# A four-layer graph network on one core: layer 2's first maxima formed beside layer 1's sums, part of the neighbour counts moved into layer 1, and the stores moved to another queue

## The chip, the cores and the metric

The kernel runs on one core of one Trainium2 chip. The metric is the time of one execution on the device in microseconds (us). The kernel before takes 3031.22 us (median of three runs, 3029.73 to 3033.5).

A core has five engines, each with its own instruction stream[...]: PE (matrix multiply, with a separate stream of weight loads), DVE (vector), ACT (scalar functions), POOL (general) and SP (here only the issue of transfers). ACT and POOL issue transfers too. The 16 DMA engines move the data. [...]

## The reference, cut to what matters

There are N = 4096 nodes with D = 256 features and a 4096 x 4096 int32 adjacency matrix with about 0.8% ones. Each layer normalises each row, takes `relu`, applies a graph operation and adds the result to `x`.

```
for layer in 0..3:   h = relu((x - mean) / sqrt(var + eps));   x = x + layer(h)

layer 0: attention over neighbours (leaky slope 0.2), a wide dense part, a gate, a norm
layer 1: a = (adj == 1);  deg = a.sum(axis=1);  (a @ h / deg) @ W.T + b
layer 2: g = h @ W;  src = g @ a[:D];  dst = g @ a[D:]
         e = src[:,None] + dst[None,:];  e = where(e > 0, e, 0.01 * e)
         elu(softmax(where(adj > 0, e, -1e12), axis=1) @ g)
layer 3: Q, K, V = h@Wq, h@Wk, h@Wv;  softmax(Q K^T + mask(adj + I)) @ V
```

In layer 2 the row maximum of the masked `e` only needs, for each row, the largest `dst` among its neighbours, because the leaky function rises everywhere.

## The kernel before, in words

The rows are cut into NT = 32 tiles of 128 rows; four tiles make a block (`BT` = `RB` = 4), so there are NB = 8 blocks. All of `x` stays on the chip as `xs`. The order of the instructions on each engine is set by the framework's scheduler, which takes the program's order as priority; the order named here is that of the built kernels. Pools with few buffers and releases of memory add waits.

**Layer 0** first runs an attention (`class Attention`), which also turns the adjacency into transposed codes and stores them in DRAM (`codesT`, one MB for each block of four row tiles and each quarter of the columns). Then comes its dense part (`dense`, lines 691 to 850), a generator for each block of rows; two blocks are in flight. `with_counts` runs a `count` (lines 681 to 692) after each step: POOL loads a 128 x 1024 piece of the adjacency as bf16 (`ask`, line 681, four buffers), and ACT reads it twice with a Sign function whose sum goes to `over` (line 689). There are 128 pieces and 256 signs; from them comes `deg`. `turn` transposes on PE, and its result is taken out of PSUM by DVE (`onto`, line 644) or ACT (`nc.scalar.copy`, line 641). `measure1` takes mean and deviation of the finished rows for layer 1, with one POOL power (line 117).

**Layer 1** (lines 862 to 938) starts with `opening`: the last four blocks of `h @ W.T` (`halves1`), in a high and a low half. `gather(t)` then loads the codes of row tile t through SP (line 902, four buffers `code`), compares them with one value on DVE (line 907, two buffers `eq` of the whole width), sums with 32 matrix products on PE (line 911, two PSUM buffers `acc`), and adds the mean to `xs` (ACT line 918, DVE lines 920 to 922).

**Layer 2** (lines 941 to 998) begins when layer 1's memory is free. POOL loads W and a (lines 187 and 194), and DVE forms W a from them (line 202). For each block, `block2` normalises (`preln`, ACT line 134), transposes (line 145) and projects (`project`, line 154, ACT line 215), which gives g, src and dst together. `reach(n)` (lines 236 and 238) takes two column tiles of the running maximum of dst over the neighbours: DVE subtracts and takes the minimum on a 128 x 512 tile in PSUM. At a block's last n it turns the result, forms two rows, and sends them through DRAM to get them to all partitions (`ab_d`, `ab_row`, lines 271 and 272). `run` then goes over eight row blocks and 16 pairs of column tiles: DVE makes `y` (line 284), POOL subtracts the code (line 288), ACT takes the exponential (line 315), PE sums (line 326). `reach` of the next block runs among them, LEAD = 3 pairs ahead.

**Layer 3** goes over 16 pairs of row tiles; `fetch3` loads codes through SP (line 1079), and the results go out through POOL (line 1177).

Of the kernel before, what the change touches and what calls it, by code (L numbers as in the profile page):

```python
# [21 lines left out]
P = 128  # L22
# [19 lines left out]
def kernel(ctx: ExitStack, tc: tile.TileContext, w: dict, out: bass.AP):  # L42
# [114 lines left out]


# [6 lines left out]
    class Attention:  # L165
        def __init__(self, outer, es, tag, slope, lag, n_y, blocks, turned, finish, side="left"):
# [3 lines left out]
            vp = outer.enter_context(tc.tile_pool(name=f"{tag}_v", bufs=1, side=side))  # L170
            self.v = vp.tile([P, NT, D + 3], F32, name="v")
            nc.gpsimd.memset(self.v[:, :, 0:1], 1.0)
            vp = es.enter_context(tc.tile_pool(name=f"{tag}_sd", bufs=1))
            self.sdst = vp.tile([P, NT], F32, name="sdst")
            self.cdst = vp.tile([P, NT], F32, name="cdst")
            self.ab_d = [
# [6 lines left out]
            self.ps_top = es.enter_context(tc.tile_pool(name=f"{tag}_top", bufs=1, space=PSUM))  # L183
        def weights(self, wp, work, wm, a_srcs, eng):
# [23 lines left out]
        def project(self, b, hT, psm, rs=None):  # L208
# [9 lines left out]
            at = ts(b, BT)  # L218
            dst = self.v[:, at, D + 2]
# [3 lines left out]
        def reach(self, n):  # L223
# [8 lines left out]
            for j in range(c, c + 2):  # L232
                code = self.turned(b, j // QT)[:, :, j % QT, :]
                dst = self.v[:, j, D + 2 : D + 3]
                if j == 0:
                    nc.vector.tensor_scalar(st["run"], code, dst, None, ALU.subtract)
                else:
                    nc.vector.scalar_tensor_tensor(  # L238
                        st["run"], code, dst, st["run"], ALU.subtract, ALU.min
                    )  # L240
            if c < NT - 2:
                return
# [98 lines left out]
    def measure1(small, b):  # L341
        at = ts(b, BT)
        mv = small.tile([P, BT, 2], F32, tag="pl_mv", name="pl_mv")
        for i in range(BT):
            stats_of(small, xs[:, b * BT + i, :], mv[:, i, :], "pl")
        rs = rstd_of(small, mv, BT, "pl", stats1[:, 0, at])
        nc.vector.scalar_tensor_tensor(
            stats1[:, 1, at], mv[:, :, 0], -1.0, rs, ALU.mult, ALU.mult
# [32 lines left out]
    with ExitStack() as l0:  # L381
# [10 lines left out]
        with ExitStack() as es:  # L392
# [18 lines left out]
            att = Attention(v0, es, "l0", 0.2, 3, 8, cuts, turned_of, finish0, "right")  # L411
# [192 lines left out]
        with ExitStack() as es:  # L604
            d = es.enter_context(tc.tile_pool(name="l0_d", bufs=1))
            AHEAD = 4
# [68 lines left out]
            asked, came = [(t, q) for t in range(NT) for q in range(NQ)], []  # L675

            def ask(n):
                for t, q in asked[len(came) : n]:

                    came.append(code_p.tile([P, QW], BF16, tag="a", name="a", bufs=AHEAD))  # L680
                    nc.gpsimd.dma_start(out=came[-1], in_=adj[ts(t, P), ts(q, QW)])

            def count(g):

                ask(g + AHEAD - 1)
                t, q = asked[g]
                for v in range(2):
                    sign = code_p.tile([P, QW], BF16, tag="sign", name="sign", bufs=1)
                    nc.scalar.activation(  # L689
                        sign, came[g], AF.Sign, bias=limits[:, v : v + 1],  # L690
                        accum_out=over[:, t, v, q : q + 1],
                    )

            def dense(b):
# [8 lines left out]
                for k in range(KD):  # L703
                    turn(
                        whT[:, k, :], [wh[:, b * BT + i, ts(k, P)] for i in range(BT)],
                        onto if k else nc.scalar.copy,
# [42 lines left out]
                turn(abT, [dt[:, i, :] for i in range(BT)], nc.scalar.copy)  # L749
# [87 lines left out]
                if b < NB - 1:  # L837
                    measure1(small, b)
# [18 lines left out]
            def with_counts(b):  # L857
                at, n = b * BT * NQ, BT * NQ
                for k, _ in enumerate(dense(b)):
                    if k < n:  # L860
                        count(at + k)
                    yield

            ask(AHEAD - 2)
            run_staggered([with_counts(b) for b in range(NB)], 16)

    with ExitStack() as es:  # L870

        code_p = es.enter_context(tc.tile_pool(name="l1_code", bufs=4))
        eq_p = es.enter_context(tc.tile_pool(name="l1_eq", bufs=2))
# [8 lines left out]
        psm = es.enter_context(tc.tile_pool(name="l1_psm", bufs=3, space=PSUM))  # L882
        ps_acc = es.enter_context(tc.tile_pool(name="l1_acc", bufs=2, space=PSUM))

        def block1(b):
            if b == NB - 1:
                measure1(small, b)
            h = work.tile([P, BT, D], F32, tag="h", name="h")
            hT = work.tile([P, KD, BW], F32, tag="hT", name="hT")
# [4 lines left out]
        nc.vector.tensor_reduce(sums, over, AX.X, ALU.add)  # L894
        rdeg = vp.tile([P, NT], F32, name="rdeg")
        nc.vector.tensor_tensor(rdeg, sums[:, :, 0], sums[:, :, 1], ALU.subtract)
        nc.vector.tensor_scalar(rdeg, rdeg, 0.5, None, ALU.mult)
        nc.vector.reciprocal(rdeg, rdeg)
        def gather(t, parts=1):
# [6 lines left out]
            eq = eq_p.tile([P, N], F32R, tag="eq", name="eq")  # L906
            nc.vector.tensor_scalar(eq, code, UNIT, None, ALU.is_equal)  # L907
            yield
            acc = ps_acc.tile([P, 2 * D], F32, tag="acc", name="acc")
            for c in range(NT):  # L910
                nc.tensor.matmul(  # L911
                    out=acc, lhsT=eq[:, ts(c, P)], rhs=v1[c // BT][:, c % BT, :, :],
# [9 lines left out]
            nc.vector.tensor_tensor(xs[:, t, :], xs[:, t, :], o, ALU.add)  # L922

# [17 lines left out]
    with ExitStack() as es:  # L941
        work2 = es.enter_context(tc.tile_pool(name="l2_work", bufs=2))

        minus = const.tile([P, 1], F32, name="minus")
        nc.gpsimd.memset(minus, -1.0)

        def finish2(at, accs, rden):

            h = work2.tile([P, RB, D], F32, tag="hp", name="hp")
            for r, acc in enumerate(accs):  # L950
                by = rden[:, r : r + 1]
                if r % 2:
                    nc.vector.tensor_scalar(
                        h[:, r, :], acc[:, 1 : D + 1], by, -1.0, ALU.mult, ALU.add
                    )
                else:
# [275 lines left out]
```

## Time and profile before

The profiled execution took 3033.89 us; its span, from the first to the last instruction, is 3032.1 us.

| Stage | from, us | to, us | PE busy, us | ACT busy, us | DVE busy, us | POOL busy, us |
|---|---|---|---|---|---|---|
| layer 0, attention | 0 | 625 | 569.5 | 351.9 | 402.8 | 368.6 |
| layer 0, dense part | 625 | 1239 | 576.8 | 496.3 | 288.0 | 275.2 |
| layer 1, opening | 1239 | 1285 | 40.0 | 18.5 | 21.0 | 7.1 |
| layer 1, sums | 1285 | 1507 | 221.8 | 14.8 | 125.8 | 6.0 |
| layer 2, before its first sum | 1507 | 1576 | 42.0 | 31.9 | 49.1 | 7.1 |
| layer 2, attention | 1576 | 2057 | 463.0 | 199.9 | 364.3 | 278.4 |
| layer 3 | 2057 | 3032 | 963.6 | 162.0 | 602.2 | 22.4 |

The table is read from the profile's stretches: the busy time of each engine between two moments of the span. A stage in which PE is busy nearly throughout can be shortened only by letting PE do less or wait less. In a group of the profile, a name such as `L911 PE acc` is a line of the code, an engine and what is written[...]. "DMA share" is the part of a stretch in which the 16 DMA engines had a packet in hand.

### The profile page before, as it was taken

What the parts mean: (1) busy time and instruction counts of PE and PEld (TensorE: products, weight loads), DVE (VectorE), ACT (ScalarE), POOL (GpSimd) and SP (SyncE); (2) the same over time, 40 slices, a digit from 0 to 9 for tenths busy, and PEclk for the clock granted to TensorE, in tenths of its full rate; (3) what the DMA queues carried; (4) which work ended last, traced back from release to release, by engine and by line L of the source; (5) the groups of instructions that cost most, each with busy time, mean ns of one, the idle gap of its engine ahead of it and who ended that gap; (6) DMA issues with size and microseconds to landing.
All of it is one profiled execution on the core that took longest, in us unless ns stands there. A gap on an engine that the chain in (4) does not pass through costs nothing.

```text
span 3032.1 us, 34952 instructions
## 1 busy us (share of the span) xinstructions
PE 2876.7 (95%) x13353; PEld 2343.2 (77%) x13353; DVE 1853.2 (61%) x3304; ACT 1275.3 (42%) x1944; POOL 964.7 (32%) x750
## 2 busy tenths in 40 slices
PE   6999999999899999899969999999999999999999
PEld 5778888866565665788758887888888888888887
DVE  5876666425444444455588878745766566566653
ACT  5766555369999972410144344443212111111211
POOL 4676665535544443100025565550000000000000
PEclk9999999999999999999979999999999999999999
DMA  6966655244444430244222222101111111111100
GB/s 144 213 146 126 140 122 141 57 69 74 77 77 75 75 53 8 97 149 147 84 105 87 84 77 77 49 18 60 63 34 61 39 34 61 35 37 61 34 7 8
DMA packets 105824, 235.21 MB, mean 78 GB/s; under 512 B 10716, under 2 KB 27096, under 8 KB 97464
## 3 DMA queue, kind: packets, MB, share of 16 engines
q0 software_dynamic: 39232, 73.30, 15.8%
q1 hardware_dynamic: 63752, 157.04, 15.0%
q10 hardware_dynamic: 2672, 2.62, 0.3%
q8 instruction: 105, 1.72, 0.2%
q14 instruction: 63, 0.52, 0.1%
HBM read 262.22 MB, written 37.81 MB: 99 GB/s over the span
## 4 chain that ended last, share of the span: by engine, by line
PE 39%; issue 31%; ACT 10%; POOL 7%; DVE 7%; DMA 4%; POOLq 0%; ACTq 0%; SPq 0%; DVEq 0%
PE acc L326 18%; PE acc L911 8%; PE mm L154 7%; POOL y L288 4%; ACT sign L689 4%; PE s L154 3%; DVE run L238 3%; PE acc L1164 2%; DVE y L284 2%; DMA ab_row<-l_ab_d 1%; DMA a<-in_adj_dram 1%; ACT y L315 1%; ACT zT L667 1%; ACT turned L449 1%; ACT t L656 1%
## 5 line engine op out<-in xcount | busy, mean ns | idle before, releaser
L326 PE MATMUL acc<-v,y 128*128 128x257 f32 x4096 | 938.0, 387 | 35.3 <-ACT hp L957 17.0
L326 PEld LDWEIGHTS acc<-v,y 128*128 128x128 f32 x4096 | 778.0, 193 | 152.0 <-ACT hp L957 21.8
L288 POOL TENSOR_TENSOR y<-y,turned 128x1024 f32<-128x1024 f32 (+1 forms) x272 | 550.1, 2035 | 339.0 <-DVE y L284 298.4
L315 ACT ACTIVATE y<-y,sdst 128x512 f32<-128x512 f32 (+1 forms) x544 | 350.7, 689 | 365.1 <-POOL y L288 364.8
L284 DVE SCALAR_TENSOR_TENSOR y<-ab_row,cdst,b 128x512 f32<-128x512 f32 (+1 forms) x544 | 368.2, 710 | 166.5 <-PE acc L326 108.1
L1164 PE MATMUL acc<-v,y 128*128 128x257 f32 x2048 | 454.5, 380 | 0.4 <-DVE rden L1172 0.4
L154 PE MATMUL s<-qT,hT 128*128 128x256 f32 x2048 | 445.2, 379 | 0.7 <-ACT qT L1112 0.7
L1157 ACT ACTIVATE y<-y 128x1024 f32<-128x1024 f32 x128 | 132.2, 1055 | 714.3 <-DVE y L1156 710.0
L154 PEld LDWEIGHTS s<-qT,hT 128*128 128x128 f32 x2048 | 389.0, 190 | 54.2 <-ACT qT L1112 1.4
L1164 PEld LDWEIGHTS acc<-v,y 128*128 128x128 f32 x2048 | 387.1, 190 | 55.9 <-issue 0.8
L238 DVE SCALAR_TENSOR_TENSOR run<-turned,v,run 128x512 f32<-128x512 bf16 (+1 forms) x527 | 379.5, 720 | 61.1 <-DMA turned<-codesT 27.0
L1177 POOL DMA_DIRECT2D out_dram<-o x32 | 17.3, 542 | 936.5 <-DVE rden L1172 933.0
L689 ACT ACTIVATE sign<-a,limits 128x1024 bf16<-128x1024 bf16 x256 | 294.0, 1148 | 16.9 <-DMA a<-in_adj_dram 11.0
L1126 DVE SCALAR_TENSOR_TENSOR y<-code,s 128x512 f32<-128x512 bf16 x256 | 175.7, 687 | 100.6 <-PE s L154 100.3
L1156 DVE TENSOR_TENSOR y<-y,top 128x1024 f32<-128x1024 f32 x128 | 146.2, 1214 | 43.0 <-PE top L1150 43.0
L1133 DVE TENSOR_TENSOR mx<-mx,y 128x512 f32<-128x512 f32 x224 | 154.8, 691 | 7.5
L449 ACT ACTIVATE turned<-cT,log_wide 128x1024 bf16<-128x1024 bf16 x128 | 141.1, 1102 | 31.7 <-PE cT L444 31.3
L154 PE MATMUL mm<-kept 128*128 128x512 f32 x288 | 137.4, 612 | 8.8 <-ACT kept L641 7.5
L911 PE MATMUL acc<-early,eq 128*128 128x512 f32 x512 | 127.1, 400 | 4.3 <-DVE early L372 2.5
L907 DVE TENSOR_SCALAR eq<-code 128x4096 fp32r<-128x4096 bf16 x32 | 73.4, 2294 | 81.6 <-PE acc L911 78.8
L911 PE MATMUL acc<-late,eq 128*128 128x512 f32 x512 | 122.7, 391 | 0.0
L911 PEld LDWEIGHTS acc<-early,eq 128*128 128x128 f32 x512 | 96.9, 190 | 27.8 <-DVE early L372 2.8
(224 smaller groups left out, 2951.3 us busy)
## 6 DMA issues: line engine op xcount, KB each, us to landing
adj_t<-in_adj_dram POOLq DMA_DIRECT2D x128, 256.0 KB, 4.7
codesT<-turned SPq DMA_DIRECT2D x32, 1024.0 KB
a<-in_adj_dram POOLq DMA_DIRECT2D x128, 256.0 KB, 4.2
code<-codesT SPq DMA_DIRECT2D x128, 256.0 KB
turned<-codesT SPq DMA_DIRECT2D x32, 1024.0 KB
code<-codesT SPq DMA_DIRECT2D x64, 512.0 KB
ab_row<-l_ab_d SPq DMA_DIRECT2D x15, 512.0 KB
xt<-in_x_dram SPq DMA_DIRECT2D x8, 512.0 KB
```

The lines of the kernel that those rows point to most:

```text
L154: nc.tensor.matmul(out=ps, lhsT=lhsT_of(k), rhs=rhs_of(k), start=(k == 0), stop=(k == n - 1))
L238: nc.vector.scalar_tensor_tensor(st["run"], code, dst, st["run"], ALU.subtract, ALU.min)
L284: nc.vector.scalar_tensor_tensor(y[:, :, k, :], st["ab"][:, 0, :, :], self.cdst[:, c + k : c + k + 1], st["b"], ALU.add, ALU.max,)
L288: nc.gpsimd.tensor_tensor(y, y, mask[:, :, c % QT : c % QT + 2, :], ALU.subtract)
L315: nc.scalar.activation(y[:, :, k, :], y[:, :, k, :], AF.Exp, bias=self.sdst[:, c + k : c + k + 1],)
L326: nc.tensor.matmul(out=acc, lhsT=y[:, r, k, :], rhs=self.v[:, c + k, 0 : D + 1], start=(c + k == 0), stop=(c + k == NT - 1),)
L449: nc.scalar.activation(ct.rearrange("p c i -> p (c i)"), ps, AF.Exp, scale=math.log(UNIT / WIDE), bias=log_wide,)
L689: nc.scalar.activation(sign, came[g], AF.Sign, bias=limits[:, v : v + 1], accum_out=over[:, t, v, q : q + 1],)
L911: nc.tensor.matmul(out=acc, lhsT=eq[:, ts(c, P)], rhs=v1[c // BT][:, c % BT, :, :], start=(c == 0), stop=(c == NT - 1),)
L1126: nc.vector.scalar_tensor_tensor(y[:, :, c : c + 2, :], st["code"][:, :, c : c + 2, :], -BIG / UNIT, ps, ALU.mult, ALU.add,)
L1133: nc.vector.tensor_tensor(mx, mx, y[:, :, c : c + 2, :], ALU.max)
L1164: nc.tensor.matmul(out=accs[r], lhsT=st["y"][:, r, c, :], rhs=v3[:, c, :], start=(c == 0), stop=(c == NT - 1),)
```

## The change

- **Counts.** `Tally` replaces `ask` and `count`. Twenty-two row tiles (`COUNTED`) are counted in layer 0's dense part, 11 pieces for each block in place of 16; the last ten tiles (40 pieces, 80 signs) are counted in layer 1, written in `gather(t)` for the tiles t up to 27. `deg` of these ten is formed tile by tile (`degrees`).
- **Dense part.** DVE takes both halves of `whT` and `abT` out of PSUM; ACT took `abT` and one half of `whT` before.
- **Layer 1.** `code` has two buffers in place of four, `eq` is split into two halves with three half buffers in place of two whole ones, and one PSUM buffer `mm` is given up (three to two), as layer 2's `run` and `top` are now held in layer 1.
- **Layer 2's dst.** After each fourth row tile of layer 1, `reach2(b)` measures the four finished tiles, normalises them on ACT (`normed2`), and lets DVE form dst as a product with the vector W a (`wa2`, spread over all partitions by two matrix products in `weights2`) and a sum along the row. It then takes the two `reach` steps of row block 0 that these columns allow; the codes for it come through SP into one buffer (`stored1`). After block 6 the normalised and turned rows of blocks 0 and 1 (`hT2`) are made.
- **Layer 2's start.** `project` no longer waits for any of this and no `reach` of block 0 is left; `top(0)` finishes block 0's maxima after its projection.
- **Stores.** SP issues the 32 stores of the result in place of POOL.

```diff
+        def count(self, g):
+            self.ask(g + self.bufs - 1)
+            t, q = self.asked[g]
+            for v in range(2):
+                sign = self.pool.tile([P, QW], BF16, tag="sign", name="sign", bufs=1)
+                nc.scalar.activation(
+                    sign, self.came[g], AF.Sign, bias=limits[:, v : v + 1],
+                    accum_out=over[:, t, v, q : q + 1],
+                )
...
-                        onto if k else nc.scalar.copy,
+                        onto,
...
-                turn(abT, [dt[:, i, :] for i in range(BT)], nc.scalar.copy)
+                turn(abT, [dt[:, i, :] for i in range(BT)], onto)
...
-        code_p = es.enter_context(tc.tile_pool(name="l1_code", bufs=4))
-        eq_p = es.enter_context(tc.tile_pool(name="l1_eq", bufs=2))
+        code_p = es.enter_context(tc.tile_pool(name="l1_code", bufs=2))
+        eq_p = es.enter_context(tc.tile_pool(name="l1_eq", bufs=3))
+        over_a = es.enter_context(tc.tile_pool(name="l1_a", bufs=AHEAD))
...
-            eq = eq_p.tile([P, N], F32R, tag="eq", name="eq")
-            nc.vector.tensor_scalar(eq, code, UNIT, None, ALU.is_equal)
+            eqs = []
+            for half in range(2):
+                eqs.append(eq_p.tile([P, N // 2], F32R, tag="eq", name="eq"))
+                nc.vector.tensor_scalar(
+                    eqs[-1], code[:, ts(half, N // 2)], UNIT, None, ALU.is_equal
+                )
+            for g in range(t * n_late // BESIDE, min((t + 1) * n_late // BESIDE, n_late)):
+                tally.count(g)
+                if g % NQ == NQ - 1:
+                    at = COUNTED + g // NQ
+                    degrees(slice(at, at + 1))
...
+            if t % BT == BT - 1:
+                reach2(t // BT)
...
+        def reach2(b):
+            if b == 0:
+                weights2()
+            measure(small, b, stats2)
+            for i in range(b * BT, b * BT + BT):
+                h = two2.tile([P, D], F32, tag="hd", name="hd")
+                normed2(h, i)
+                junk = two2.tile([P, D], F32, tag="junk", name="junk")
+                nc.vector.tensor_tensor_reduce(
+                    junk, h, wa2[0], 1.0, 0.0, ALU.mult, ALU.add, att2.own_dst[:, i : i + 1]
+                )
+            att2.slopes(ts(b, BT))
+            for n in range(2 * b, 2 * b + 2):
+                att2.reach(n)
+            if b == NB - 2:
+                for k in range(2):
+                    hT2[k] = turn2(k, pst)
...
             def block2(b):
-                h = work.tile([P, BT, D], F32, tag="h", name="h")
-                preln(small, xs[:, ts(b, BT), :], h)
-                yield
-                hT = transposed_block(work, pst, h, "hT")
+                hT = hT2.pop(b) if b in hT2 else turn2(b, pst)
                 yield
-                att.project(b, hT, psm)
+                att2.project(b, hT, psm)
                 yield
-                for n in range(2 * b, 2 * b + 2 if b < NB - 1 else PPB + LEAD):
-                    att.reach(n)
-
-            run_staggered([block2(b) for b in range(NB)], 2)
-
-        att.run(es, LEAD, 5)
+            blocks = [block2(b) for b in range(NB)]
+            for _ in blocks.pop(0):
+                pass
+            att2.top(0)
+            run_staggered(blocks, 1)
+            for n in range(PPB, PPB + LEAD):
+                att2.reach(n)
+        att2.run(es, LEAD, 5)
...
-                nc.gpsimd.dma_start(out=out[ts(t, P), :], in_=o)
+                nc.sync.dma_start(out=out[ts(t, P), :], in_=o)
```

## The prediction

> **What bounds the kernel now.** I read the stretches of the span first, stage by stage, then the chain that ended last between 1507 and 1641 us, then single groups.
>
> ```profile
> 625.00:1239.00 614.00, 576.80 (x2132) 370.72 (x2131) 288.00 (x643) 496.25 (x793) 275.19 (x254) 0.97 0.40 63
> 1285.00:1507.00 222.00, 221.75 (x961) 180.43 (x962) 125.76 (x199) 14.82 (x37) 6.04 (x6) 1.00 0.41 124
> 1507.00:1576.00 69.00, 41.99 (x200) 33.66 (x199) 49.12 (x98) 31.93 (x71) 7.07 (x7) 0.79 0.31 122
> ```
>
> Columns: stretch, length, busy us of PE, weight loads, DVE, ACT, POOL, then granted clock, DMA share, GB/s. PE sets the time almost everywhere. The hole is the third stretch: from layer 1's last sum to layer 2's first, PE works 42 of 69 us at a clock of 0.79. The chain tells why:
>
> ```profile
> 1507.09 0.89 PE tp L145 x8
> 1511.23 9.84 DMA a<-in_L_gnn_a_dram
> 1522.09 13.07 PE mm L154 x48
> 1550.92 3.66 PE mm L154 x16
> 1556.02 0.77 DVE run L238
> 1570.75 1.41 DVE y L284 x2
> 1572.46 2.13 POOL y L288
> 1574.61 0.73 ACT y L315
> 1575.39 34.48 PE acc L326 x144
> ```
>
> Layer 2's weights come late (PE resumes at 1522), eight blocks are projected until 1558, and only then do block 0's maxima end. Turning them, two transfers and y take until 1575.39.
>
> **The change, part by part.**
>
> *Layer 2's start.* Removed from here: the weights' load and the `reach` steps of block 0. What stays on PE: eight projections of 3.66 us (the x16 row) and six turned blocks of 0.89 us, 34.6 us. Before, the eight projections with five turned blocks among them took 1522.09 to 1558.06, 36.0 us, so the eight need 36.9 with the sixth. ACT is nearly as full: 32 row copies at 0.38, 24 `relu` at 0.55, six evictions at 0.59 and four late `relu` for the last tiles make 31 us. Those four wait for the last tiles' deviation (below) with PE's evictions queued behind them; I add 1.5 us. With the first y's exponential 1.5 more: 1507 + 36.9 + 1.5 + 1.5 = 1546.9, against 1575.4. **-28.5 us.**
>
> The other path must be shorter. After the last sum: mean added (0.37 + 0.42 + 0.48 + 0.42, with hops 2.0), deviation (0.43 + 0.18 + 0.17 + POOL 1.02 + 0.16, with hops 2.4), `relu` and four row sums (3.0), four `reach` at 0.77 (3.1): 1517.5. From there the old tail, from the end of `run` (1559.4) to PE's start (1575.4), is 16 us. The row's two transfers go through SP behind loads of codes (1520 to 1530: DMA share 1.01 at 427 GB/s), 3 to 5 us more. Row ready and exponential possible at about 1537 to 1539, 8 us before PE is free. So y runs further ahead than before, which bears on the end of layer 2's first row block:
>
> ```profile
> 1630.00:1640.00 10.00, 6.03 (x28) 4.94 (x26) 7.33 (x16) 6.98 (x11) 10.00 (x5) 0.98 0.30 105
> 1640.00:1650.00 10.00, 9.80 (x31) 8.07 (x32) 6.41 (x8) 4.20 (x7) 4.41 (x3) 0.68 0.14 48
> 1650.00:1660.00 10.00, 10.00 (x47) 8.76 (x47) 8.19 (x12) 4.00 (x6) 6.07 (x4) 1.00 0.14 60
> ```
>
> PE gets 28 and 31 records through where 47 is normal: 35 records, 7.4 us, lost because DVE was not ahead. Eight more us of lead could remove all of it or, if DVE spends them on evictions, nothing. I take half: **-4 us** (0 to -7).
>
> *Dense part.* Per block here: 40 signs in the built order, before and after, until they run out. A sign takes 1.148 + 0.190 us, in a row one each 1.27.
>
> ```profile
> L689 ACT ACTIVATE sign<-a,limits 128x1024 bf16<-128x1024 bf16 x256 | 294.0, 1148 | 16.9 <-DMA a<-in_adj_dram 11.0
> 879.60:954.30 74.70, 70.67 (x258) 45.47 (x257) 34.97 (x80) 69.16 (x112) 37.26 (x36) 0.95 0.49 77
> 1104.60:1175.50 70.90, 68.01 (x255) 44.33 (x254) 35.69 (x80) 33.05 (x52) 27.02 (x17) 0.98 0.07 15
> ```
>
> Moving 80 signs takes 80 x 1.27 = 102 us from ACT, but PE is busy 70.7 of 74.7 us beside them. With few signs left a block takes 70.9 to 71.6, with 40 it takes 75.1 (mean of the five intervals between the table loads ahead of zT from 708 to 1084). The signs end after 4.4 intervals in place of 6.4, so two intervals are shortened: 2 x 3.5 = 7 us. The evictions moved to DVE (16 at 0.69) spare ACT's delay (PE waited 0.9 us for each) where signs stand in front, and where none do they lengthen PE's wait for whT (2.3 us at 1127.7) by about 0.7: +1. **-6 us** (-18 to +3).
>
> *Layer 1's opening.* DVE's first instruction for layer 2's weights stands ahead of the first eq, and waits for W and a through POOL. `w_L_gnn_WT`, issued at the same place before, took 7.8 us; alone, a load of this size took 3.2. So that eq starts at 1248 to 1253 (1247.4 before), with eight evictions queued behind. The half eq (1.15) gives back 1.1; two `mm` buffers for three and 16 signs among the ACT evictions cost up to 1.27 a step. **+2 us** (-1 to +8).
>
> *Layer 1's sums.* PE needs 7.41 us a tile (222/30). DVE for four tiles: eq 9.2, mean and statistics 7.7, degrees 1, `reach2` 6, together 24 of 29.6 us. A half eq may begin 7.4 us ahead of its use; going through DVE's order at a `reach2`, the latest half is done 3 us early. ACT: signs come at 20 to 21 for four tiles, 26 us, with `lo` and `relu` 31 of 29.6, until the 80 are gone at about tile 13. `lo` waits behind them, and PE for `lo`, but a sum has two buffers, 5 us of slack: nothing yet. POOL's powers queue behind its loads, and those wait for signs, which only passes the same lag on.
>
> The scarcest is DMA. One piece costs 1.75 us of the 16 engines (0.49 x 74.7, less 1.5 for x, over 20 pieces), a code tile 3.5 (0.47 x 7.41), `stored1` 0.4. Per tile 2.6 x 1.75 + 3.5 + 0.4 = 8.4 against 7.41: 1.0 x 12 tiles = 12 us, less 5 for the two sums and 3 for the four piece buffers. **+4 us** (0 to +14). SP's four new loads wait for the previous one's use, issued a block earlier; the first waits for layer 0's memory with code tile 2 behind it, needed 35 us later.
>
> [...]
>
> ```profile
> L907 DVE TENSOR_SCALAR eq<-code 128x4096 fp32r<-128x4096 bf16 x32 | 73.4, 2294 | 81.6 <-PE acc L911 78.8 <-DMA code<-codesT 2.9
> ```
>
> [...] Before, POOL issued nothing beside it, [...] I take 0.
>
> *Stores.* SP's fetch in layer 3 comes once in 56 us, and stores ahead of it are done by then: nothing. At the end POOL's second issue came at 3028.63, 2.5 us after the first ended, and landed 2.0 later; SP issues at its own 0.4 each: **-2.5 us** (-4 to 0).
>
> **Sum.** -28.5 - 4 - 6 + 2 + 4 - 2.5 = -35 against the profiled span of 3032.1, 2997; its own execution took 3033.9, 2.7 above the median of the runs. From 3031.2: **2996 us.**
>
> **Rivals.**
> - *The lag in layer 1 reaches PE.* For it: the 8.4 us, and everything from `lo` to the powers in one line. If neither buffers help nor the opening: +12, +8, +8 in place of +6: 3012 to 3022, I say 3014. Against it: 93% of ACT and 59% of DMA time there is free today. 0.18.
> - *More gain.* All of the 7.4, a start at PE's 34.6, and dense -15: 2977. For it: slower PE clock after each wait (0.95 in the dense intervals). Against it: whT's wait is DVE's. 0.20.
> - *Layer 2's start stays bound.* The row arrives after the projections, behind the loads in SP's queue, or ACT's order holds PE: first sum at 1556, 3005 to 3009. 0.12.
> - *Slower.* Code loads share the DMA engines with the pieces, with two buffers for four. If each of 13 tiles waits for its code, layer 1 decides at 35/13 = 2.7 us a tile, 10.1 us: a code load (4.4 us at 1242.9) would have to take over 12 us from eq to eq. At 11.5 us a tile: 3050. 0.04.
> - *The signs do not move or the weights stay late*: the built order shows both moved; 0.01.
>
> **How the numbers follow.** The case of the sum has 0.45, and its own range is 2986 to 3006. With the rivals, 2976 to 3015 leaves 0.2 out. Faster by over 0.2% (about what three runs of this kernel tell from no change: below 3025) 0.93, within it 0.03, slower 0.04.
>
> **What would show it.** Layer 2's first sum about 40 us after layer 1's last (69 before), at full clock. Layer 1's 30 tiles in 222 to 230 us, DMA share near 1 and ACT full until tile 13. Dense intervals of 75 for four, then 71. Last store issued by SP within 1 us of DVE. The prediction is wrong if PE waits in layer 1 for `lo` or eq at every tile, or if PE's stop at 1630 stays.

## The result, and the profile after

The changed kernel takes 2998.55 us (median of four runs, 2995.66 to 3001.03); the kernel before took 3030.47 us beside it (four runs). The ratio is 0.9894, 95% interval 0.9882 to 0.9906. The forecast was 2996 us, with a range of 2976 to 3015. The profiled execution of the changed kernel took 2998.89 us; its span is 2997.0, against 3032.1 before: 35.1 us less, where the sum of the prediction had 35. By the medians the gain is 31.9 us; the profile of before was one of the slower executions (3033.89 us), and that the two sums agree to 0.1 us is chance.

The agreement says little about the terms. To see them, the span is cut at events that both kernels have: the first table load of ACT inside the dense part, the last tanh of the dense part, the first and the last sum of layer 1, the first and the last sum of layer 2, and the first scores of layer 3.

| Stage, us | before | after | change | predicted |
|---|---|---|---|---|
| layer 0 up to the first table load | 651.6 | 648.4 | -3.2 | 0 |
| dense part, first table load to last tanh | 577.6 | 562.7 | -14.9 | -6 |
| layer 1's opening, last tanh to first sum | 21.2 | 26.0 | +4.8 | +2 |
| layer 1's sums | 256.7 | 261.0 | +4.3 | +4 |
| layer 2's start, last sum of layer 1 to first of layer 2 | 68.3 | 40.2 | -28.1 | -28.5 |
| layer 2, first to last sum | 480.2 | 480.2 | 0.0 | -4 |
| layer 3's opening, to its first scores | 44.8 | 50.2 | +5.4 | not in the sum |
| layer 3's scores, sums and stores | 931.8 | 928.4 | -3.4 | -2.5 |
| span | 3032.1 | 2997.0 | -35.1 | -35 |

So the large term held, and five others were off by 2.8 to 8.9 us, with signs that cancel. These are the stretches of the changed kernel that answer to those shown of before (stretch, length, busy us of PE, weight loads, DVE, ACT, POOL, then granted clock, DMA share, GB/s):

```profile
606.90:1220.90 614.00, 584.68 (x2203) 376.31 (x2202) 297.69 (x659) 392.70 (x616) 253.81 (x216) 0.99 0.29 46
1271.80:1498.30 226.50, 224.93 (x987) 182.53 (x986) 162.19 (x364) 109.97 (x203) 29.08 (x37) 1.00 0.66 178
1498.10:1538.30 40.20, 35.40 (x182) 29.61 (x180) 36.74 (x68) 29.59 (x69) 4.66 (x4) 1.00 0.50 196
1568.30:1578.30 10.00, 5.76 (x29) 4.74 (x28) 8.79 (x17) 4.26 (x7) 4.57 (x3) 0.97 0.21 75
1578.30:1588.30 10.00, 10.00 (x41) 8.49 (x40) 8.26 (x12) 0.59 (x1) 0.64 (x1) 0.86 0.25 84
852.20:927.00 74.80, 70.50 (x259) 44.21 (x257) 37.84 (x82) 69.44 (x110) 38.10 (x38) 0.98 0.51 78
996.50:1066.30 69.80, 67.90 (x257) 43.29 (x256) 36.02 (x82) 21.46 (x31) 26.26 (x16) 1.00 0.02 8
```

The reader sees ACT lose 104 us of work in the dense part (496.3 to 392.7) and gain 95 in layer 1 (14.8 to 110.0). Layer 2's start is 40.2 us long at full clock, with PE busy in 35.4 of them. A dense interval without signs takes 69.8 us. And the stop of PE near the end of layer 2's first row block, 28 and 31 records where 47 are normal before (each of these products leaves two records, 4096 for the 2048 of L368), is still there: 29 and 41.

The chain that ended last, over the new start of layer 2 (start us, us, engine, tile, line):

```profile
1496.94 1.15 PE acc L1006 x5
...
1500.89 1.01 POOL stats L117
...
1502.12 1.09 ACT hd L934 x2
...
1503.53 3.76 PE mm L154 x16
...
1508.55 0.44 PE top L289 x4
...
1516.12 0.69 DVE hT L109
1516.81 0.67 DVE run L275
...
1526.64 0.60 DVE hT L109
...
1527.38 3.73 PE mm L154 x16
...
1532.64 0.60 ACT b L324
...
1533.26 1.42 DVE y L326 x2
...
1534.80 2.14 POOL y L330
...
1538.26 6.96 PE acc L368 x31
```

The 9.84 us for the load of `a` and the wait for the maxima are gone. The last tiles' deviation (POOL, DVE) comes first, then the projections on PE; block 0's maxima are turned at 1508.55 in the midst of them. From 1516 to 1527 the chain runs through DVE, which takes the turned rows `hT` out of PSUM between the `reach` steps of row block 1 (`run`). The 40.2 us are 35.4 us of PE's work and three waits: 0.6 us for ACT, 2.3 for `hT` from DVE, and 1.9 at the end for the first `y`. The logits `b` come late: SP issues the load of their row at 1514.83, but ACT copies it at 1532.64, behind its copies for the projections.

### The profile page after: what moved, and what is told of

It is laid out like the page before. It is cut to its first block, busy times and chain, and to the rows that moved or that the text cites. A ratio compares the mean times of both kernels' runs of the same rounds, so it can differ in the third digit from the quotient of the medians.

```text
span 2997.0 us, 35132 instructions
## 1 busy us (share of the span) xinstructions
PE 2864.1 (96%) x13357; PEld 2334.0 (78%) x13357; DVE 1878.5 (63%) x3456; ACT 1282.4 (43%) x1961; POOL 954.4 (32%) x718
## 4 chain that ended last, share of the span: by engine, by line
PE 63%; ACT 9%; issue 8%; POOL 7%; DVE 7%; DMA 5%; POOLq 0%; ACTq 0%; DVEq 0%; SPq 0%
PE acc L368 16%; PE acc L1273 15%; PE s L154 15%; PE mm L154 9%; PE acc L1006 5%; POOL y L330 4%; ACT sign L180 4%; DVE run L275 3%; DVE y L326 2%; DMA a<-in_adj_dram 1%; DMA ab_row<-l_ab_d 1%; ACT y L357 1%; DMA turned<-codesT 1%; ACT turned L493 1%; PE q_ps L154 1%
## 5 line engine op out<-in xcount | busy, mean ns | idle before, releaser
L368 PE MATMUL acc<-v,y 128*128 128x257 f32 x4096 | 932.8, 386 | 24.5 <-ACT hp L917 16.0
L368 PEld LDWEIGHTS acc<-v,y 128*128 128x128 f32 x4096 | 774.6, 192 | 139.6 <-ACT hp L917 21.3
L275 DVE SCALAR_TENSOR_TENSOR run<-turned,dst,run 128x512 f32<-128x512 bf16 x248 | 186.7, 753 | 42.1 <-DMA turned<-codesT 37.4
L275 DVE SCALAR_TENSOR_TENSOR run<-turned,v,run 128x512 f32<-128x512 bf16 (+1 forms) x279 | 192.9, 691 | 24.2 <-ACT turned L493 18.5
L173 POOL DMA_DIRECT2D a<-in_adj_dram x128 | 76.1, 596 | 190.8 <-ACT sign L180 158.2
```

The costliest lines, as they stand in the source:

```text
L275: nc.vector.scalar_tensor_tensor(st["run"], code, dst, st["run"], ALU.subtract, ALU.min)
L368: nc.tensor.matmul(out=acc, lhsT=y[:, r, k, :], rhs=self.v[:, c + k, 0 : D + 1], start=(c + k == 0), stop=(c + k == NT - 1),)
```

## The experiments

Every run is compared with the kernel before on the same chip. Times are medians. The stages of every profiled span, with the edges of the table above:

| Run | to table load | dense | opening | sums | layer 2's start | layer 2 | layer 3's opening | rest | span |
|---|---|---|---|---|---|---|---|---|---|
| before | 651.6 | 577.6 | 21.2 | 256.7 | 68.3 | 480.2 | 44.8 | 931.8 | 3032.1 |
| after | 648.4 | 562.7 | 26.0 | 261.0 | 40.2 | 480.2 | 50.2 | 928.4 | 2997.0 |
| e1 weights of layer 3 early | 653.1 | 564.4 | 26.2 | 259.1 | 40.2 | 479.4 | 44.4 | 928.4 | 2995.3 |
| e2 counts back | 650.1 | 568.7 | 25.4 | 258.0 | 39.9 | 477.0 | 50.2 | 928.4 | 2997.7 |
| e3 evictions back | 647.4 | 563.6 | 26.5 | 260.8 | 40.2 | 477.2 | 50.0 | 928.4 | 2994.0 |
| e4 W a deferred | 648.5 | 563.3 | 19.2 | 266.8 | 40.2 | 479.2 | 50.2 | 928.4 | 2995.8 |
| e5 before, stores on SP | 648.4 | 572.5 | 20.9 | 256.8 | 68.5 | 478.5 | 44.8 | 928.2 | 3018.6 |
| e6 e1 + e4 + signs late | 647.5 | 563.5 | 19.2 | 260.6 | 40.2 | 478.4 | 44.4 | 928.4 | 2982.2 |
| e7 e6 + pieces late | 652.3 | 560.3 | 19.2 | 266.0 | 40.2 | 479.2 | 44.4 | 928.4 | 2990.1 |
| e8 e1 + e4 + no counts in layer 1 | 647.6 | 573.5 | 19.2 | 259.5 | 39.9 | 478.0 | 46.1 | 928.5 | 2992.3 |
| e9 e6 + 8 code buffers, 7 y | 653.0 | 561.7 | 19.2 | 259.9 | 39.9 | 487.7 | 44.4 | 928.5 | 2994.3 |
| e10 e6, maxima in layer 2 | 652.4 | 559.2 | 19.2 | 258.4 | 51.3 | 481.2 | 46.1 | 928.2 | 2996.0 |
| e11 e6 + 9 y | 648.7 | 558.7 | 19.2 | 259.9 | 40.2 | 499.3 | 44.5 | 928.5 | 2998.9 |
| e12 e11 + 16 tiles counted first | 653.8 | 554.4 | 19.2 | 265.6 | 40.2 | 491.7 | 44.4 | 928.4 | 2997.7 |

How far two executions of the same code differ can be read from it. The part up to the first table load is alike in all of them and takes 647.4 to 653.8 us, so the -3.2 us of the first table lies within the spread. The dense part is the same code in eight of them (after, e1, e4, e6, e7, e9, e10, e11): 558.7 to 564.4, mean 561.7. What follows repeats within about 3 us where the code is the same, with one exception, layer 2 in e11 and e12 (below).

### Layer 3's opening: the weights are late (e1)

The pools of layer 2 are now opened ahead of layer 1's, and what layer 3 lays in the freed memory falls on other tiles. The issue of layer 3's first weight in the kernel before, in the changed kernel, and in e1:

```profile
2031.93 0.76 POOL L96 DMA_DIRECT2D w_L_gnn_Wq<-in_L_gnn_Wq_dram  x1 [0.30 <-POOL y L288]
```

```profile
2018.73 0.78 POOL L96 DMA_DIRECT2D w_L_gnn_Wq<-in_L_gnn_Wq_dram  x1 [13.23 <-PE acc L368]
```

```profile
1998.86 0.78 POOL L96 DMA_DIRECT2D w_L_gnn_Wq<-in_L_gnn_Wq_dram  x1 [0.30 <-POOL y L330]
```

Before, it follows POOL's last subtraction and is 23.6 us ahead of layer 2's last sum (2055.5). In the changed kernel it waits 13.2 us for PE, until that last sum.

```diff
+            pad = es.enter_context(tc.tile_pool(name="l3_pad", bufs=1))
+            pad.tile([P, 8 * D], F32, name="pad")
             wp = es.enter_context(tc.tile_pool(name="l3_w", bufs=1))
```

> An unused gap of 8 KB for each partition is laid ahead of layer 3's weights, so that they lie where layer 2's codes lay and not where PE still reads; nothing else changes. Theory (the weights are late): in the changed kernel they are issued 13.2 us later, after layer 2's last sum, and the stretch from that sum to layer 3's first scores is 50.2 us against 44.8 before; with the gap it is 44 to 46 and the time 2993 to 2994. Rival (the statistics of the last rows on DVE and POOL set that stretch): it stays at 49 to 50, and the time at 2998.

Measured: 2990.48 us, ratio 0.988 (0.9862 to 0.9899). Layer 3's opening takes 44.4 us. The theory of the late weights holds for the stretch; the time is 2.5 us below the range that it gave. The statistics do not set this stretch. The 5.4 us are a side effect of where memory lies, which no line of the diff's core tells.

### The dense part: signs and evictions (e2, e3, e5)

```diff
-    COUNTED = 22
+    COUNTED = 32
```

> All 32 row tiles are counted in layer 0 again (no signs and no pieces in layer 1); evictions stay on DVE. Theory A (the 18 us that the dense part gained come from the signs that left it): its last tanh goes back from 1211 to 1224 to 1229; layer 1's sums fall from 261 to 257, its opening stays at 26 because layer 2's weights hold the first eq, not the signs; the time is 3007 to 3012. Theory B (they come from the evictions that left ACT): the last tanh stays at 1211 to 1216, and the time is 2994 to 2999. If the signs hold layer 1's opening, that falls to 21 and both times are 5 us less.

Measured: 3001.1 us, ratio 0.9912 (0.9896 to 0.9928). The last tanh comes at 1218.8, between the two theories, and so does the time. Layer 1's sums fall to 258.0. Layer 1's opening stays at 25.4 us without any sign, so the signs alone do not hold the first sum there.

```diff
-                        onto,
+                        onto if k else nc.scalar.copy,
...
-                turn(abT, [dt[:, i, :] for i in range(BT)], onto)
+                turn(abT, [dt[:, i, :] for i in range(BT)], nc.scalar.copy)
```

> The two evictions of each dense block go back to ACT; the counts stay moved. Theory A (the signs that left give the dense part's gain): the last tanh stays at 1209 to 1213, the time at 2997 to 3000. Theory B (the evictions give it): the last tanh at 1220 or later, the time 3007 or more. The prediction had put 7 us on the signs and a loss of 1 on the evictions: by it 2997.5.

Measured: 3002.52 us, ratio 0.9913 (0.9894 to 0.9931); the last tanh at 1210.99 is as theory A had it, the time lies between the two.

The times of the two don't tell them apart from each other or from the changed kernel; the stages do. With e5 (below), e8 and the kernel before, the dense part is known for all four combinations:

| Dense part, us (in brackets: slots at half clock in it, explained below) | evictions on ACT | evictions on DVE |
|---|---|---|
| 32 tiles counted here | 577.6 (10), 572.5 (6) | 568.7 (3), 573.5 (6) |
| 22 tiles counted here | 563.6 (4) | 558.7 (0) to 564.4 (4), mean of eight 561.7 (2) |

Taking 80 signs away shortens the dense part by about 9 us with the evictions on DVE and 11 with them on ACT, clear of the spread. Moving the evictions shortens it by 4 us at most, and there the cells overlap. Theory A is right in kind. From before to after the gain is 10 to 15 us, where 6 had been put.

Why an interval with signs is at times longer is seen in e5, the kernel before with the stores moved. Its five full intervals of the same work take 73.7, 76.6, 73.3, 76.8 and 72.1 us at granted clocks of 1.00, 0.94, 1.00, 0.93 and 1.00. PE's waits in the second (long) and in the third (short) interval (waiting instruction, releaser, us in total, times, longest):

```profile
PE tp L640 <- DVE whT L644: 2.6, 1, 2.6
PE mm L154 <- ACT kept L641: 2.1, 1, 2.1
PE tp L640 <- ACT whT L641: 2.1, 1, 2.1
```

```profile
PE tp L640 <- DVE whT L644: 1.9, 1, 1.9
PE mm L154 <- ACT kept L641: 0.9, 1, 0.9
PE tp L640 <- ACT whT L641: 0.9, 1, 0.9
PE tp L640 <- ACT t L656: 0.2, 1, 0.2
```

What such a wait cost depended on where it lay in time. In all fourteen profiles each stretch at half clock lasts 3.41 us or a multiple of it (but for a last one that the end of the trace cuts off), and all those of one execution lie on one grid of slots of 3.41 us, whose place changes from execution to execution. Here are the slots around one and the same wait of PE for `whT` in the changed kernel (2.07 us) and in e7 (2.08 us), whose dense part is the same code:

```profile
966.80:970.21 3.41, 1.34 (x13) 1.10 (x12) 2.67 (x7) 0.59 (x1) 2.73 (x2) 1.00 0.19 67
970.21:973.63 3.42, 3.42 (x16) 3.04 (x15) 1.17 (x3) 1.06 (x2) 2.75 (x3) 0.50 0.00 0
```

```profile
968.36:971.77 3.41, 2.68 (x19) 2.23 (x17) 2.25 (x11) 0.58 (x1) 1.40 (x2) 1.00 0.66 154
971.77:975.18 3.41, 2.06 (x16) 1.93 (x17) 2.64 (x6) 0.49 (x1) 3.41 (x2) 1.00 0.00 0
975.18:978.60 3.42, 3.42 (x16) 2.82 (x15) 2.25 (x5) 1.38 (x2) 3.23 (x2) 1.00 0.02 5
```

In the changed kernel the wait lies within one slot; PE is busy for 0.39 of it, and the next slot runs at half clock. In e7 the border of two slots cuts the wait, neither falls below 0.60, and the clock stays at 1.00. Between 650 and 1200 us of the fourteen profiles, a slot at full clock with PE busy, by the profile, for less than 0.45 of it was followed by half clock in 35 of 36 cases, a slot with more in none of 2173. In the profiles of before and after, the nine slots ahead of a half-clock slot are busy 0.24 to 0.44, the 300 others at full clock 0.46 or more. In e5's long interval the slots on which it turned are busy 0.41 and 0.33, and in the short one the lowest is 0.49:

```profile
819.05:822.47 3.42, 1.40 (x13) 1.16 (x11) 2.62 (x11) 2.46 (x4) 1.03 (x1) 1.00 0.96 227
822.47:825.88 3.41, 1.11 (x4) 0.71 (x4) 1.21 (x2) 2.63 (x5) 2.88 (x2) 0.50 0.37 68
894.15:897.56 3.41, 1.66 (x14) 1.35 (x12) 2.61 (x9) 3.31 (x7) 1.61 (x2) 1.00 1.00 219
```

The slots account for the spread of the dense part. The eight runs with the same code there took 558.7 and 559.2 us with no slot at half clock, 560.3 with one, 561.7 with two, 562.7 to 563.5 with three and 564.4 with four: about 1.4 us a slot. Taken out at that price (an estimate), the cells of the table become 563.6 and 564.1, 564.5 and 565.1, 558.0, and 558.9. So the signs themselves are worth about 6 us and the evictions a loss of about 1, within the spread, and the rest of the gain is slots: ten or six before, three after. How many slots one execution has is in part luck: these eight had none to four.

```diff
-                nc.gpsimd.dma_start(out=out[ts(t, P), :], in_=o)
+                nc.sync.dma_start(out=out[ts(t, P), :], in_=o)
```

> The kernel before with one edit: SyncE issues the 32 stores. Theory: the stretch from layer 3's first scores to the end falls from 931.8 to 928.4 us, as in the changed kernel, because POOL's second issue at the end is late; everything else stays, and the time is 3026 to 3028. Rival (that gain belongs to other parts of the change): the stretch stays at 931 to 932, the time at 3029 to 3031. It also shows the dense part of the kernel before a second time: 575 to 580 us from the first table load to the last tanh if the 577.6 of the first profile is typical, 570 or less if that was a slow draw.

Measured: 3027.2 us against 3031.15, ratio 0.9988 (0.9979 to 0.9996); the last stretch takes 928.2 us in place of 931.8. The theory holds. The dense part took 572.5 us, between the two cases that were expected; this profile is of the fastest of the run's seventeen executions (3020.42 us). Before, at the end, and the changed kernel, at the end:

```profile
3025.57 0.54 POOL L1177 DMA_DIRECT2D out_dram<-o  x1 [27.33 <-DVE rden L1172]
3028.63 0.54 POOL L1177 DMA_DIRECT2D out_dram<-o  x1 [2.52 <-issue]
```

```profile
2993.60 0.93 SPq L1286 DMA_DIRECT2D out_dram<-o  x2
```

SP issues both within 0.93 us; POOL's second came 3.1 us after its first.

### Layer 1's opening: two waits side by side (e4, e6, e7, e8)

The opening of the changed kernel in the timeline (start us, us, engine, line, operation, tiles; in brackets the idle time before it and what ended it):

```profile
1226.62 0.57 POOL L228 DMA_DIRECT2D a<-in_L_gnn_a_dram  x1
...
1234.28 0.42 DVE L236 CUSTOM_DVE_ANT_0 junk<-w,a 128x256 f32<-128x256 f32 x1 [6.30 <-DMA a<-in_L_gnn_a_dram]
...
1235.15 1.23 DVE L995 TENSOR_SCALAR eq<-code 128x2048 fp32r<-128x2048 bf16 x1
...
1237.08 2.05 PE L1006 MATMUL acc<-early,eq 128*128 128x512 f32 x4 [9.14 <-issue]
...
1239.17 1.15 ACT L180 ACTIVATE sign<-a,limits 128x1024 bf16<-128x1024 bf16 x1 [10.61 <-DMA a<-in_adj_dram]
```

DVE stands 6.3 us at the first part of W a, with the first eq behind it; ACT stands 10.6 us at the first sign, with the evictions of layer 1's opening behind it. e4 takes the first wait away:

```diff
             for k in range(KD):
+                if self.own_dst is not None:
+                    nc.vector.tensor_scalar(
+                        w2[:, k, D : D + 2], xs[:, 1, 0:2], 0.0, None, ALU.mult
+                    )
                 for v in range(2):
```

> The product W a of layer 2 is made to wait for row tile 1 of layer 1 (one 128x2 instruction of DVE ahead of each pair reads that tile), so that the first eq no longer stands behind the load of a. Theory: in the changed kernel DVE waits 6.3 us there, PE 9.1 us; the stretch from the dense part's end to the first sum falls from 26 to 19 to 21, and the time to 2992 to 2994. Rival (the signs and POOL's queue hold the opening anyway): the first sum comes earlier but the 30 tiles after it take as much longer, and the time stays at 2997 to 2999.

Measured: 2993.71 us, ratio 0.9886 (0.9869 to 0.9903). The first sum comes after 19.2 us in place of 26.0, and the sums take 266.8 in place of 261.0: of 6.8 us gained, 5.8 are given back. By the stages the rival holds; the time lies in the range of the theory, but its interval overlaps that of the changed kernel and can't decide. In the timeline of ACT in e4:

```profile
1241.22 1.15 ACT L180 ACTIVATE sign<-a,limits 128x1024 bf16<-128x1024 bf16 x1 [11.95 <-DMA code<-codesT]
...
1242.37 0.56 ACT L107 COPY hT<-tp 128x512 f32<-128x512 f32 x1
```

The sign waits 11.95 us, and the eviction that PE needs comes right after it. (The releaser named is a code load; the sign itself reads a piece that is loaded at the same time.) e6, which also has the edits of e1 and e4, holds the signs, not the first pieces, until row tile 1 is done, and spreads the pieces over the 26 tiles after it (LATE is 2):

```diff
+            if t == LATE:
+                tally.bias = one2.tile([P, 2], F32, name="limits1")
+                nc.vector.scalar_tensor_tensor(
+                    tally.bias, xs[:, t - 1, 0:2], 0.0, limits, ALU.mult, ALU.add
+                )
```

> W a deferred and layer 3's weights early (both as before), and the signs of layer 1 made to wait for row tile 1 (their bias is formed from it); the first pieces are still loaded in the opening. Theory (in the run with W a deferred, a sign waited 11.9 us for its piece at the head of ACT's queue, with an eviction for PE behind it): opening 19 to 20 and sums 258 to 261 us, 278 to 280 together against 286 to 287, and a time of 2983 to 2986. Rival (the scarce thing is the DMA engines, loaded with pieces, codes and weights at once): together 284 or more, the time 2988 to 2991.

Measured: 2985.98 us, ratio 0.9849 (0.9834 to 0.9864). Opening and sums take 279.8 us together, against 287.0 in the changed kernel and 278.0 before. The theory of the two waits holds. This is the fastest kernel of the study: 12.6 us below the median of the changed one, with an interval that lies wholly below that one's.

```diff
+                if self.hold is not None and len(self.came) <= self.bufs:
+                    nc.vector.tensor_scalar(
+                        self.came[-1][:, 0:2], self.hold, 0.0, None, ALU.mult
+                    )
                 nc.gpsimd.dma_start(out=self.came[-1], in_=adj[ts(t, P), ts(q, QW)])
```

(`hold` is a part of row tile 1, so the load waits for it; the edits of e6 are in it too.)

> As the run with the signs late, but the loads of the first four pieces wait for row tile 1 too. By the theory of the signs nothing more is gained: 278 to 280 us for opening and sums, 2983 to 2986. By the theory of the DMA engines this run alone brings it down: 277 to 280 where the other one stays at 284 or more.

Measured: 2988.46 us, ratio 0.9855 (0.9838 to 0.9871). Opening and sums take 285.2 us, so neither expectation is met. The theory of the DMA engines falls, as holding the first pieces back as well does not help, but the theory of the signs had 278 to 280; the sums take 266.0. PE waits 5.8 us for eq there, against 1.1 in e6; 3.6 of them are for tile 1's code at 1238. Why that code comes later there is open.

> W a deferred and layer 3's weights early, and all 32 row tiles counted in layer 0, so that layer 1 has neither signs nor pieces. By both theories opening and sums take 276 to 279 us (278.0 before the change), the dense part 567 to 570, and the time is 2986 to 2990. If they take 283 or more, what is left of the loss in layer 1 comes from the two code buffers, the two mm buffers or dst, not from the counts.

(The edit is e1, e4 and COUNTED = 32.) Measured: 2994.03 us, ratio 0.9877 (0.9862 to 0.9892). Opening and sums take 278.7 us, as expected; the dense part (573.5) and the time are longer than expected. So once both waits are out of the way, 80 signs and 40 pieces beside the sums cost 279.8 - 278.7 = 1.1 us, little more than the 0.7 by which e6, e9 and e11 differ there, and leaving them in layer 0 costs about ten.

### What layer 2's start consists of (e10)

```diff
-            for n in range(2 * b, 2 * b + 2):
-                att2.reach(n)
...
             for _ in blocks.pop(0):
                 pass
-            att2.top(0)
+            for n in range(PPB):
+                att2.reach(n)
```

> As the run with the signs late, but the 16 steps of row block 0's maxima are taken in layer 2 again, after its memory is free; W a, dst and the turned rows of two blocks stay in layer 1. It splits the 28.3 us that layer 2's start gained. Theory A (steps and everything else were one chain, and the steps on DVE are most of it: 32 at 0.77 = 24.6 us, with evictions and four loads of codes ahead): layer 2's first sum comes 55 to 65 us after layer 1's last, against 40.2. Theory B (what counted was that the weights and dst came late; the steps fit beside the projections): 42 to 50. Layer 1's sums, rid of the steps and of their loads, fall from 260.6 to 257 or 258.

Measured: 2996.07 us, ratio 0.9892 (0.9873 to 0.9911). The stretches from layer 1's last sum to layer 2's first, in e10 and in e6:

```profile
1489.15:1540.40 51.25, 35.52 (x182) 29.46 (x180) 46.41 (x80) 29.73 (x69) 4.09 (x4) 0.90 0.38 154
```

```profile
1490.80:1531.00 40.20, 35.41 (x182) 29.61 (x181) 36.69 (x68) 29.54 (x69) 4.61 (x4) 1.00 0.49 196
```

PE does the same 35.5 us of work; with the 16 steps back (two instructions each) DVE is busy 46.4 of 51.25 us, its `run` is 41% of the chain, and PE waits 11.0 us for the first `y`. Between the two theories, nearer to B: of the 28.1 us about 11 come from the steps and the other 17 from what e10 leaves in layer 1, the weights, W a, dst and the turned rows of two blocks, which it does not separate. The steps cost layer 1 2.2 us (sums 260.6 with them, 258.4 without).

### Layer 2's head start (e9, e11)

```diff
-        turned_p = es.enter_context(tc.tile_pool(name="l2_turned", bufs=7))
+        turned_p = es.enter_context(tc.tile_pool(name="l2_turned", bufs=8))
...
-    att2 = Attention(l2, "l2", 0.01, 3, 8, cuts2, None, finish2)
+    att2 = Attention(l2, "l2", 0.01, 3, 7, cuts2, None, finish2)
```

> As the run with the signs late, with eight buffers for layer 2's codes in place of seven and seven for y in place of eight [...]. Layer 2 took 480.2 us from its first to its last sum before and after, so the head start was lost again. Theory: at each row block's end a code load waits in SP's queue for POOL's last subtraction from the buffer it reuses, DVE waits for that load at a step of the maxima (2.3 us at 1601 in the changed kernel), and the reciprocals on which PE's next sums depend stand behind it; with one more buffer layer 2 takes 458 to 468 us and the time is 2966 to 2976. Rival (DVE and POOL have no more to give: y and maxima together fill their time): 476 to 480, and 2984 to 2988 or, with y short of a buffer, more.

Measured: 2996.19 us, ratio 0.9891 (0.9869 to 0.9913). Layer 2 is 9 us longer, not shorter. DVE still waits 31.9 us for codes (36.8 in e6), so one buffer more takes little of that wait away. The edit mixes one buffer more of codes and one less of y, and DVE's and ACT's built order in layer 2 is another than in e6; it can't separate these.

> As the run with the signs late (2985.98 us), with nine buffers for y in place of eight. The run with seven had lost 8 to 9 us in layer 2 although it had one more buffer for codes. Theory (the lead that the four engines have over each other in layer 2 is bounded by y's buffers): layer 2 takes 470 to 475 us against 478.4, and the time is 2978 to 2983. Rival (eight are enough, and what the seventh run lost was a threshold; the end of a row block is set by the codes' loads and the release of PSUM): 477 to 480 and 2984 to 2988.

(The edit is 9 in the place of the 8.) Measured: 3002.99 us, ratio 0.9918 (0.9905 to 0.9931). Layer 2 takes 499.3 us, 21 more. Both expectations miss. The scheduler, given a ninth buffer, writes another order on DVE, ACT and PE: more y run ahead and the next block's maxima come later. ACT's waits in layer 2, e11 and e6:

```profile
ACT abT_sb L306 <- PE abT L304: 43.0, 7, 7.2
```

```profile
ACT abT_sb L306 <- PE abT L304: 7.8, 7, 1.5
```

ACT waits 43.0 us for the turned maxima of the seven later blocks in place of 7.8. Of the 21 us, 8.8 are PE busy longer with the same products (467.4 us against 458.6), with ten slots at half clock in layer 2 in place of five. So the number of y's buffers comes with another order, and neither 7 nor 9 says what buffers alone would do.

> As the run with nine buffers, with 16 row tiles counted in layer 0 in place of 22, so 128 signs and 64 pieces in layer 1. By the dense intervals (73.8 us with signs, 69 to 70 without) the 48 signs that leave are 1.2 intervals, 4 to 5 us less; if layer 1 has room (its 80 signs cost 1 us when they come after the opening), 1 to 2 of these are lost there: 3 us faster than the run with nine buffers. Rival (the DMA engines, 8.4 us of work a tile against 7.4 while pieces are loaded, or ACT, 31 of 29.6 us, have no slack for 20 tiles in a row): layer 1's sums go from 260 to 266 or more, and it is no faster or slower.

(COUNTED = 16.) Measured: 3000.51 us, ratio 0.9914 (0.9900 to 0.9929). The dense part gives the expected 4.3 us (558.7 to 554.4), and layer 1's sums take 265.6 us in place of 259.9: as the rival had it, there is no room for 64 pieces and 128 signs. PE waits 3.2 us behind signs and 1.8 for `o`, which points to ACT more than to the DMA engines. The time is 2.5 us lower all the same, because layer 2, with the same order of instructions as in e11, is 7.6 us shorter: it has seven slots at half clock in place of ten, and PE is busy 462.1 us in place of 467.4.

## Why the prediction was right, and which of its steps were not

The forecast of 2996 us, its range and its sign were right. By its own steps:

- *Layer 2's start, -28.5.* Right: -28.1, and by the path it named: the last tiles' deviation (0.6 us, where 1.5 was taken), the projections, the first exponential (1.9, where 1.5 was taken). In e10, where the other path (the maxima) is made long again, it decides, as the working feared for a late row.
- *End of layer 2's first row block, -4.* Wrong: 0.0. PE's stop stays, which the prediction itself had named as a sign of being wrong. Thirty-five records were missing before; after, 18, 6 and 10 in 1568 to 1578, 1578 to 1588 and 1598 to 1608, 34 in all. The step that failed is "So y runs further ahead than before": the eight us of lead did not arise. The load of block 0's row and ACT's copy of it, before and after:

```profile
1565.94 0.33 SPq L272 DMA_DIRECT2D ab_row<-l_ab_d  x1
...
1569.86 0.59 ACT L282 COPY b<-ab_row 128x512 f32<-128x512 f32 x1 [5.21 <-DMA ab_row<-l_ab_d]
```

```profile
1514.83 0.32 SPq L314 DMA_DIRECT2D ab_row<-l_ab_d  x1
...
1532.64 0.59 ACT L324 COPY b<-ab_row 128x512 f32<-128x512 f32 x1
```

  Before, the copy follows the issue by 3.9 us, and ACT has waited for the row. After, the row is asked for early enough, but the copy follows 17.8 us later, with no wait of ACT just ahead of it: ACT's order has it behind the copies for the projections, and DVE takes 28 instructions of row block 1's maxima ahead of the first `y`. The first `y` starts 4.6 us ahead of the first sum before and 5.0 after, and at the first sum one `y` has passed POOL in both. Later DVE stands 5.2 us, from 1553.9, at the first step of row block 2's maxima (counted from 0), until ACT has copied those of block 1 (one PSUM buffer `run` for both); the steps then come between the y, and block 1's rows `ab` are formed behind them at 1577. PE waits 4.2 us for these rows with its sums behind (0.7 before). What would remove the stop is open.
- *Dense part, -6.* The two terms were right by the estimate above, about 6 us for the signs (7 were taken) and a loss of about 1 for the evictions. What the sum left out is the clock: it took ACT's delay as 0.9 us each and put nothing on the slots at half clock, which fell from ten (six in e5) to three at about 1.4 us each. "Slower PE clock after each wait" stood among the rivals, with 0.20. The profile of before was the longer of two draws (577.6 us, 572.5 the second time), so the gain is 10 to 15.
- *Layer 1's opening, +2.* The mechanism was right (the first eq behind W a, W a behind POOL's load of `a`), and the size at the upper end: +4.8. That the wait of the first sign lies beside it was not seen. Opening and sums take 286.0 us with the sign's wait alone (e4, against 279.8 in e6) and 283.4 with W a's alone (e2, against 278.7 in e8), so either would have done most of the harm.
- *Layer 1's sums, +4.* The size was right and the cause was not. DMA at 8.4 us a tile against 7.4 was to reach PE; in e6 the sums pass at a DMA share of 0.88 to 1.07 for 100 us, from 1275 to 1375, with PE at 44 to 47 records in every 10 us. Of the 3.9 us left in e6, 2.2 go with the maxima (e10) and 1.1 with the counts (e8). At 64 pieces and 128 signs (e12) there is a limit, but PE's waits name the signs.
- *POOL's issues beside an eq, taken at 0.* Right for PE, which waited 1.3 us for eq in all, though POOL itself took longer. Two issues of pieces and an eq in the changed kernel's timeline:

```profile
1254.78 1.56 POOL L173 DMA_DIRECT2D a<-in_adj_dram  x1 [8.04 <-ACT sign L180]
...
1255.00 2.36 DVE L995 TENSOR_SCALAR eq<-code 128x2048 fp32r<-128x2048 bf16 x2
...
1259.97 0.54 POOL L173 DMA_DIRECT2D a<-in_adj_dram  x1 [3.63 <-ACT sign L180]
```

  From 1237 to 1380, 22 issues that meet no eq take 0.53 to 0.59 us; the 14 that do take 0.92 on average and up to 1.56, while eq takes 1.22 to 1.23 in all 64 cases. That is 14 x 0.38 = 5.3 us, all on POOL, which has room (30.8 us busy of these 143).
- *Stores, -2.5.* Right in kind, -3.4.
- *What the sum did not have:* +5.4 us at layer 3's opening. The working asked which loads wait for layer 0's memory at layer 1's start and did not ask the same of layer 3 when it moved layer 2's pools.

Against the rivals (the 2977 of "more gain" is 2978 by its own terms): "layer 2's start stays bound" and "slower" did not happen. "The lag in layer 1" came in part (+9.1 for opening and sums, where 6 was taken), and "more gain" came in part, in the dense part. The range held because these two ran against each other, and the closeness of 2996 to 2998.55 is to that extent luck.

## What to carry to other kernels

A wait was worth here what stood behind it in its engine's queue: with the signs at the head of ACT's queue opening and sums took 286.0 us (e4), with the same signs behind row tile 1 279.8 (e6). And where two such waits lay side by side, taking one away showed only the other (287.0 to 286.0 in e4). When pools are opened earlier, list for every later load which tiles it now lies on. And judge a sum of terms by stages with common edges: here the total agreed to 0.1 us while five of eight stages were off by about 3 us or more.

## What was not expected of the hardware

In the fourteen profiles PE fell to half clock for 3.41 us or a multiple of it, on one grid of slots for each execution. A slot in the dense part in which PE was busy for less than 0.45 was followed by one at half clock in 35 of 36 cases. A wait of 2.07 us that lay within one slot was followed by 3.41 us at half clock (the changed kernel), and one of 2.08 us that a border cut was not (e7). The place of the grid changed from execution to execution. With that, the dense part of one and the same code varied by 5.7 us, with none to four slots at half clock, while layer 2's start, which has none, took 39.9 to 40.2 us in the eleven profiles that share its code, and layer 3 with stores on SP 928.2 to 928.5 in all of them.
